# Where TensorE issues D·xs and the sums over states in a selective-scan kernel

## The chip, the cores and the metric

The kernel runs on one core of a Trainium2 chip. A core has five engines that run side by side[...]: TensorE (PE in the profile, its weight loads PEld), VectorE (DVE), ScalarE (ACT), GpSimd (POOL) and SyncE (SP), which here issues every DMA. The metric is the device time of one execution in microseconds, as a median of several executions.

## The reference, cut to what matters

Two layers are computed on x of shape (2, 256, 256, 128) in float32. The first is an attention along rows, which the change leaves alone. The second is a selective scan (Mamba-like) over the 256 × 256 tokens of each of the two images, with 256 inner channels and 16 states a channel:

```python
dA  = exp(delta[:, :, :, None] * A[None, :, None, :])
dBx = (delta * xs)[..., None] * Bs            # along the tokens
h   = dA_t * h + dBx_t                        # the recurrence, one token after another
y_t = sum_n h[:, :, n] * c_t[:, n]            # sum over the 16 states
y   = y + Ds * xs
out = (layernorm(y) * silu(z)) @ out_proj_w.T # plus the residual
```

xs, z, Bs, Cs and delta come from the normalised input by a projection with a 3 × 3 depthwise convolution (one set of nine matmuls here), a SiLU and small projections.

## The kernel before, in words

After the attention, which takes the first 2.67 ms, comes the scan stage. It works through 128 **steps** (two images, 64 steps each); a step is 4 rows of 256 tokens, T = 1024 tokens. A step is cut into NU = 32 **units**, one per **slot** of the schedule: two halves h of 128 channels, in each four groups m of four states, in each four groups q of 32 channels. A unit fills 128 partitions with 32 channels × 4 states. So a half is 16 units (NM), and four consecutive units (NQ) share m.

For a unit t the engines do this:

- `decay` (ACT, L956): da = exp(delta · A), written one slot ahead. Two buffers, da0 and da1.
- `drive` (POOL, L966): hb = (delta·xs)·B for two units at once, three buffers.
- `scan` (DVE, L978): the recurrence over 1024 tokens.
- `product` (DVE, L992): yc = h · C, except for the pairs that `POOLED` names (units 2, 3, 6, 7, 10, 11, 18, 19, 26, 27 of a step), whose product `products` (L1001) does on POOL two slots later. yc has four buffers of two units each.
- `add_up` (PE, L1023): for four units at once, 16 matmul records with the constant matrix `sel` add the four states of yc into y in PSUM. For the first group of a half (m = 0) the old `add_up` first loads xr (the half's xs, L1012) and puts D·xs into y with a diagonal matrix (L1016, 4 records).
- `y_out` (ACT, L1036): y goes to SBUF after a half's last group.
- `remember` (ACT, L983): keeps the last column of h for the next step.

A product of unit t writes into a yc buffer that the group of units around t − 8 used; it waits until that group's `add_up` has read it.

Beside the units, each slot carries **pieces** of other work, placed by `at(...)`: the projection of a later step (`project`: transposes t_ps L658, convolution taps u_ps L676, z_ps L702, xd_ps L726, dt_ps L744, each followed one or more slots later by the ACT instruction that empties its PSUM buffer: xn L663, xs L687, sz L713, xd L739, delta L755) and the end of an earlier step (`finish_row`, one row of 256 tokens every 8 slots: yt L828, ACT statistics and scaling L840 to L852, yd L863, gating on DVE L871, o_ps L875 and L879, and the ACT copy ob L889). All the projection's PE pieces share one PSUM buffer (pool `ps_p`, bufs = 1), so each waits until ACT has emptied the one before. The finish pieces share another (`ps_f`).

The order on PE, ACT, DVE and POOL is written out by hand: inside `tc.manual_schedule` the loop over t issues, for each slot, what the body names, top to bottom, and each engine runs its own part in that order. Only SP, the queue of the DMAs, is ordered by the framework's scheduler. `slots` holds for each slot a pair of lists: pieces of other engines, and pieces of PE. In the old loop a slot's PE work was all pieces of PE first, then the sums. The sums of a group of units u to u+3 come in slot u+5, or u+6 if the last pair's product is POOL's. Counted within a step, the groups 0, 4, 8, 16 and 24 are summed in slots 6, 10, 14, 22 and 30; groups 12, 20 and 28 have no POOL product in their last pair and are summed in slots 17, 25 and 1 (of the next step). Slot 17 also holds a z_ps piece, slot 25 four transposes, slot 1 the second xd_ps piece. Groups 0 and 16 open a half, so D·xs stood in slots 6 and 22, directly ahead of the sums and behind the ninth convolution tap.

The PE pieces of slots 0 to 3, which the prediction follows, are: slot 0 yt and the first xd_ps; slot 1 the second xd_ps; slot 2 dt_ps; slot 3 the first three taps of a convolution. ACT empties the first xd_ps in slot 1, the second in slot 2, dt_ps in slot 3, in each case behind that slot's `decay` and the finish pieces, and ahead of `remember`:

```python
        for t, i in ((40, 0), (41, 1)):
            at(base + t, states, i, pe=True)
            at(base + t + 1, states_out, i)
```

Of the kernel before, what the change touches and what calls it, by code (L numbers as in the profile page):

```python
# [8 lines left out]
F32 = mybir.dt.float32  # L9
# [6 lines left out]
P = 128  # L16
# [5 lines left out]
def attn_then_ssm_kernel(  # L22
# [26 lines left out]
    nc = tc.nc  # L49
# [8 lines left out]
    TB = 512  # L58
# [63 lines left out]
    d_diag = const.tile([P, NH, P], F32, name="d_diag")  # L122
# [3 lines left out]
    NQ = P // CQ  # L126
# [7 lines left out]
    with tc.tile_pool(name="prep", bufs=1) as prep, tc.tile_pool(  # L134
        name="prep2", bufs=3
# [14 lines left out]
        for g in range(NCG):  # L150
            for m in range(NSG):
                nc.sync.dma_start(
                    out=alog_d[:, :, g, m],
                    in_=A_logs[g * CQ : (g + 1) * CQ, m * SR : (m + 1) * SR],
# [101 lines left out]
    with tc.tile_pool(name="st", bufs=1) as stp, tc.tile_pool(  # L256
        name="st_x", bufs=6
# [20 lines left out]
    with ExitStack() as actx:  # L278
# [242 lines left out]
        end = B * NA  # L521
# [59 lines left out]
    T = R * W  # L581
    NSTEP = H // R
    NB = T // TB
# [4 lines left out]
    NM = NQ * NSG  # L588

    POOLED = (2, 6, 10, 18, 26)  # L590
    s1 = ctx.enter_context(tc.tile_pool(name="s1", bufs=1))
# [5 lines left out]
    ps_y = ctx.enter_context(tc.tile_pool(name="ps_y", bufs=1, space=PSUM))  # L597
# [7 lines left out]
    slots = {}  # L605
# [9 lines left out]
    given = {}  # L615
# [296 lines left out]
    def unit(t):  # L912

        k, i = divmod(t, NU)
        h, i = divmod(i, NM)
        m, q = divmod(i, NQ)
        return k, h, m, q
# [3 lines left out]
    def fetch(t):  # L921
        k, h, m, q = unit(t)
        v = given[k]
        if q == 0:

            for name, row in (("bb", m * SR), ("cc", NS + m * SR)):
                tl = repeats[name, k, h, m] = s2.tile([P, T], F32, name=name)
                nc.sync.dma_start(
                    out=tl, in_=v["bc"][row : row + SR, :].partition_broadcast(CQ)
                )  # L930
        if m == 0:

            for name in ("delta", "du"):
                if name == "delta":
                    tl = s5.tile([P, T], F32, name="delta_r")
                elif q % 2 == 0:
                    pair = spreads["pair", k, h, q] = s3.tile([P, 2, T], F32, name="du_r")
                    tl = pair[:, 0, :]
                else:
                    tl = spreads["pair", k, h, q - 1][:, 1, :]  # L940
                spreads[name, k, h, q] = tl
                nc.sync.dma_start(
                    out=tl,
                    in_=v[name][h, q * CQ : (q + 1) * CQ, :]
                    .unsqueeze(1)
                    .to_broadcast([CQ, SR, T]),
                )

    def pooled(t):
        return t % NU - t % 2 in POOLED  # L950

    def decay(t):
        k, h, m, q = unit(t)
        da = units[t]["da"] = ps_d.tile([P, T], F32, name=f"da{t % 2}")
        g = h * NQ + q
        nc.scalar.activation(  # L956
            da, spreads["delta", k, h, q], AF.Exp, scale=a_neg[:, g, m : m + 1]
        )

    def drive(t):  # L960

        k, h, m, q = unit(t)
        hb = s3.tile([P, 2, T], F32, name="hb")
        units[t] = {"pair": hb, "hb": hb[:, 0, :]}
        units[t + 1] = {"hb": hb[:, 1, :]}
        nc.gpsimd.tensor_tensor(  # L966
            hb,
            spreads["pair", k, h, q],
            repeats["bb", k, h, m].unsqueeze(1).to_broadcast([P, 2, T]),
            ALU.mult,  # L970
        )

    def scan(t):
        k, h, m, q = unit(t)
        u = units[t]
        st = states_of[steps[k][0]][:, h * NQ + q, m : m + 1]
        u["h"] = u["hb"] if pooled(t) else u["da"]
        nc.vector.tensor_tensor_scan(u["h"], u["da"], u["hb"], st, ALU.mult, ALU.add)  # L978

    def remember(t):  # L980
        k, h, m, q = unit(t)
        st = states_of[steps[k][0]][:, h * NQ + q, m : m + 1]
        nc.scalar.copy(st, units[t]["h"][:, T - 1 : T])  # L983

    def product(t):
        k, h, m, q = unit(t)
        u = units[t]
        if t % 2 == 0:
            yc = s4.tile([P, 2, T], F32, name="yc")
            for i in range(2):  # L990
                units[t + i]["yc"] = yc[:, i, :]
        nc.vector.tensor_tensor(u["yc"], u["h"], repeats["cc", k, h, m], ALU.mult)  # L992

    def products(t):

        k, h, m, q = unit(t)
        hb = units[t]["pair"]
        yc = s4.tile([P, 2, T], F32, name="yc")
        for i in range(2):
            units[t + i]["yc"] = yc[:, i, :]  # L1000
        nc.gpsimd.tensor_tensor(  # L1001
            yc, hb, repeats["cc", k, h, m].unsqueeze(1).to_broadcast([P, 2, T]), ALU.mult
        )

    outs = {}

    def add_up(t):

        k, h, m, _ = unit(t)
        if m == 0:  # L1010
            xr = s1.tile([P, T], F32, name="xr")
            nc.sync.dma_start(out=xr, in_=given[k]["xs"][h])  # L1012
            y = outs["y"] = ps_y.tile([P, T], F32, name="y")
            for i in range(NB):
                cols = slice(i * TB, (i + 1) * TB)
                nc.tensor.matmul(  # L1016
                    y[:, cols], d_diag[:, h, :], xr[:, cols], start=True, stop=False
                )
        y = outs["y"]
        for i in range(NB):  # L1020
            cols = slice(i * TB, (i + 1) * TB)
            for q in range(NQ):
                nc.tensor.matmul(  # L1023
                    y[q * CQ : (q + 1) * CQ, cols],
                    sel,
                    units[t + q]["yc"][:, cols],
                    start=False,
                    stop=(m == NSG - 1),
                )
        for q in range(NQ):  # L1030
            del units[t + q]

    def y_out(t):
        k, h, _, _ = unit(t)
        ys[k, h] = s2.tile([P, T], F32, name=f"ys{h}")
        nc.scalar.copy(ys[k, h], outs["y"])  # L1036
# [4 lines left out]
    end = len(steps) * NU  # L1041
# [7 lines left out]
    with tc.manual_schedule(engines=engines):  # L1049
        for t in range(min(slots), max(slots) + 1):  # L1050
            if 0 <= t + AHEAD < end:
                fetch(t + AHEAD)
            if 0 <= t < end and t % (NU * NSTEP) == 0:
                st = s1.tile([P, NCG, NSG], F32, name="state")
                nc.gpsimd.memset(st, 0.0)
                states_of[steps[t // NU][0]] = st
            if 0 <= t + 3 < end and t % 2:
                drive(t + 3)
            if 0 <= t - 2 < end and t % 2 == 0 and pooled(t - 2):
                products(t - 2)  # L1060
            if 0 <= t + 1 < end:
                decay(t + 1)
            if 0 <= t < end:
                scan(t)
                if not pooled(t):
                    product(t)
            if 0 <= t - 7 < end and unit(t - 7)[2:] == (NSG - 1, 0):
                y_out(t - 7)
            for pieces in slots.pop(t, ()):
                for piece, args in pieces:  # L1070
                    piece(*args)
            for u in (t - 6, t - 5):
                if 0 <= u < end and u % NQ == 0 and (u == t - 6) == pooled(u + NQ - 1):
                    add_up(u)
            if 0 <= t < end:
                remember(t)

# [36 lines left out]
```

## Time and profile before

| | us |
|---|---|
| median of 3 executions | 16321.47 (16320.95 to 16323.75) |
| the profiled execution | 16311.47 |
| its span | 16309.7 |
| scan stage, first scan to last scan | 2671.6 to 16251.3 |
| DVE busy in the span | 14627.3 (90%) |
| PE busy | 13759.1 (84%) |
| POOL busy | 13051.0 (80%) |
| ACT busy | 10765.8 (66%) |

Inside the scan stage the shares are higher than over the span: from 8000 to 9000 us DVE is busy for 957, POOL for 940, PE for 835 and ACT for 693 us of 1000. The profile's granted TensorE clock has two values in this kernel, 1.0 and 0.5; its mean over the span is 0.941. A row of the table of groups names line, engine, operation and tiles, then the count, the busy time in us and the mean of one in ns, then the engine's idle time just before such instructions and what ended most of it. In the timeline a row is start, duration, the instruction, and in brackets the idle time before it with its releaser.

### The profile page before, as it was taken

To read this page: it belongs to the slowest core of one execution; us is meant where nothing else is said; L and a number is where in the kernel's file an instruction comes from. 1 tells how busy PE (TensorE), PEld (TensorE's weight loads), DVE (VectorE), ACT (ScalarE), POOL (GpSimd) and SP (SyncE) were. 2 spreads that over 40 slices of the span, in tenths; PEclk is the share of its full clock that TensorE was granted. 3 is DMA by queue.
4 is the path that set the end of the run, shared out by engine and by line. 5 is a ranking of instruction groups with operands and counts; after the bars stand their busy time and mean duration, and the time that the engine had idled before them with its cause. 6 is when DMAs were issued, how large, how long until landed. Compare 5 with 4: busy or idle time off the path is not lost. (4 is left out here: it accounts for less than half of the span.)

```text
span 16309.7 us, 178677 instructions
## 1 busy us (share of the span) xinstructions
PE 13759.1 (84%) x59451; PEld 7060.9 (43%) x59451; DVE 14627.3 (90%) x12484; ACT 10765.8 (66%) x20003; POOL 13051.0 (80%) x3216
## 2 busy tenths in 40 slices
PE   6999997888888888888888888888888888888886
PEld 5877883333333333333333333333333333333333
DVE  7665555999999999999999999999999999999998
ACT  3555554666666666666666666666666666666665
POOL 0111114999999999999999999999999999999997
PEclk8999998999999999999999999999999999999998
DMA  4322223666666666666666666666666666666665
GB/s 184 133 90 79 92 78 142 239 233 233 240 235 230 236 233 233 236 239 231 230 236 234 230 234 231 235 232 234 238 238 231 231 234 234 235 240 233 228 237 179
DMA packets 1428912, 3452.16 MB, mean 212 GB/s; under 512 B 119784, under 2 KB 711184, under 8 KB 1407504
## 3 DMA queue, kind: packets, MB, share of 16 engines
q1 hardware_dynamic: 1427984, 3440.73, 60.6%
q8 instruction: 467, 7.65, 0.2%
q14 instruction: 461, 3.78, 0.1%
HBM read 2752.41 MB, written 687.88 MB: 211 GB/s over the span
## 5 line engine op out<-in xcount | busy, mean ns | idle before, releaser
L966 POOL TENSOR_TENSOR hb<-du_r,bb 128x2048 f32<-128x2048 f32 x2048 | 9259.2, 4545 | 521.8 <-DVE da L978 456.4
L978 DVE TENSOR_TENSOR_SCAN da<-da,state,hb 128x1024 f32<-128x1024 f32 x2816 | 6606.2, 2346 | 137.4 <-ACT da L956 134.5
L676 PE MATMUL u_ps<-xn,w_tap 128*128 128x512 f32 x9216 | 4537.7, 641 | 657.4 <-ACT sz L713 433.7
L956 ACT ACTIVATE da<-delta_r,a_neg 128x1024 f32<-128x1024 f32 x4096 | 4588.3, 1120 | 93.0 <-ACT state L983 1.5
L992 DVE TENSOR_TENSOR yc<-da,cc 128x1024 f32<-128x1024 f32 x2816 | 3449.1, 1225 | 439.3 <-PE y L1023 277.0
L1001 POOL TENSOR_TENSOR yc<-hb,cc 128x2048 f32<-128x2048 f32 x640 | 2902.2, 4535 | 346.0 <-DVE hb L978 176.7
L676 PEld LDWEIGHTS u_ps<-xn,w_tap 128*128 128x128 f32 x9216 | 1792.6, 204 | 3099.4 <-issue 2065.9
L978 DVE TENSOR_TENSOR_SCAN hb<-da,state,hb 128x1024 f32<-128x1024 f32 x1280 | 2959.8, 2338 | 113.0 <-ACT da L956 113.0
L983 ACT COPY state<-da 128x1 f32<-128x1 f32 x2816 | 447.5, 159 | 3103.2 <-DVE yc L992 3094.6
L1023 PE MATMUL y<-yc,sel 128*32 128x512 f32 x16384 | 2192.7, 654 | 18.1 <-POOL yc L1001 18.1
L435 POOL TENSOR_TENSOR x1g<-xc,bo_all 128x512 f32<-128x512 f32 x256 | 315.7, 1274 | 1839.8 <-DVE stats L484 1838.9
L828 PE MATMUL yt<-centre,ys 128*128 128x256 f32 x4096 | 1067.1, 405 | 610.1 <-ACT ob L889 610.1
L385 ACT ACTIVATE e<-s_ps,nmx 128x256 f32<-128x256 f32 x1024 | 477.0, 475 | 968.6 <-DVE nmx L376 952.4
L828 PEld LDWEIGHTS yt<-centre,ys 128*128 128x128 f32 x4096 | 762.0, 196 | 797.7 <-ACT ob L889 707.5
L1023 PEld LDWEIGHTS y<-yc,sel 128*32 128x32 f32 x16384 | 452.6, 115 | 1499.1 <-issue 1318.1
L744 PE MATMUL dt_ps<-xd,w_dt 8*128 8x512 f32 x1024 | 685.4, 754 | 227.6 <-ACT delta L755 128.9
L702 PE MATMUL z_ps<-xn,w_z 128*128 128x512 f32 x1024 | 568.2, 636 | 332.3 <-ACT sz L713 241.2
L879 PE MATMUL o_ps<-w_out,szr 128*128 128x128 f32 x4096 | 798.0, 277 | 0.0
L879 PE MATMUL o_ps<-w_out,yg 128*128 128x128 f32 x4096 | 797.4, 277 | 0.0
L352 DVE TENSOR_TENSOR v<-v_ps,bv_all 128x512 f32<-128x512 f32 x256 | 177.0, 692 | 590.8 <-PE v_ps L345 590.8
L879 PEld LDWEIGHTS o_ps<-w_out,yg 128*128 128x128 f32 x4096 | 668.7, 194 | 27.6
L773 POOL TENSOR_TENSOR xs<-delta,xs 128x1024 f32<-128x1024 f32 x256 | 598.8, 2364 | 97.3 <-ACT delta L763 97.3
(133 smaller groups left out, 16531.0 us busy)
## 6 DMA issues: line engine op xcount, KB each, us to landing
bb<-bc_d SPq DMA_DIRECT2D x1024, 512.0 KB, 4.6
cc<-bc_d SPq DMA_DIRECT2D x1024, 512.0 KB, 4.1
delta_r<-delta_d SPq DMA_DIRECT2D x1024, 512.0 KB, 6.0
du_r<-du_d SPq DMA_DIRECT2D x1024, 512.0 KB, 5.5
sz_d<-sz SPq DMA_DIRECT2D x128, 1024.0 KB, 6.8
szr<-sz_d SPq DMA_DIRECT2D x512, 256.0 KB, 5.4
xs_d<-xs SPq DMA_DIRECT2D x128, 1024.0 KB, 8.7
xr<-xs_d SPq DMA_DIRECT2D x256, 512.0 KB, 5.4
```

Source lines behind the costliest of these rows:

```text
L676: nc.tensor.matmul(o["u"], w_tap[:, h, tap, :], xn[:, i * RB + dy : i * RB + dy + RB, dx : dx + W], start=(tap == 0), stop=(tap == 8),)
L702: nc.tensor.matmul(o["z"], w_z[:, h, :], xn[:, 1 + i * RB : 1 + (i + 1) * RB, 1 : W + 1], start=True, stop=True,)
L744: nc.tensor.matmul(o["dt"], w_dt[:, h, :], o["xd"][0:DR, i * TB : (i + 1) * TB], start=True, stop=True,)
L773: nc.gpsimd.tensor_tensor(du, o["delta"][:, h, :], du, ALU.mult)
L828: nc.tensor.matmul(o["yt"][:, j, :], ys[k, h][:, t0 + j * P : t0 + (j + 1) * P], centre[:, (1 - h) * P : (1 - h) * P + DI], start=(h == 0) ...
L879: nc.tensor.matmul(o["o"][:, j, :], o[by][:, h, j * P : (j + 1) * P], w_out[:, i, h, :], start=False, stop=(j == WT - 1 and h == NH - 1 an ...
L956: nc.scalar.activation(da, spreads["delta", k, h, q], AF.Exp, scale=a_neg[:, g, m : m + 1])
L966: nc.gpsimd.tensor_tensor(hb, spreads["pair", k, h, q], repeats["bb", k, h, m].unsqueeze(1).to_broadcast([P, 2, T]), ALU.mult,)
L978: nc.vector.tensor_tensor_scan(u["h"], u["da"], u["hb"], st, ALU.mult, ALU.add)
L992: nc.vector.tensor_tensor(u["yc"], u["h"], repeats["cc", k, h, m], ALU.mult)
L1001: nc.gpsimd.tensor_tensor(yc, hb, repeats["cc", k, h, m].unsqueeze(1).to_broadcast([P, 2, T]), ALU.mult)
L1023: nc.tensor.matmul(y[q * CQ : (q + 1) * CQ, cols], sel, units[t + q]["yc"][:, cols], start=False, stop=(m == NSG - 1),)
```

## The change

Two things move on PE; nothing is added to the computation and nothing is left out.

- D·xs and its load leave `add_up` for a new `start_up`, which is issued in slot 5 (and 21) behind that slot's PE pieces, one slot earlier than before. That puts it ahead of the ninth tap of the convolution, which is in slot 6 (and 22).
- Sums of a group whose last pair has no POOL product (slots 17, 25, 1) are issued ahead of the slot's PE pieces instead of behind them. Sums with a POOL product stay behind the pieces.

```diff
+    def start_up(t):
+
+        k, h, _, _ = unit(t)
+        xr = s1.tile([P, T], F32, name="xr")
+        nc.sync.dma_start(out=xr, in_=given[k]["xs"][h])
+        y = outs["y"] = ps_y.tile([P, T], F32, name="y")
+        for i in range(NB):
+            cols = slice(i * TB, (i + 1) * TB)
+            nc.tensor.matmul(y[:, cols], d_diag[:, h, :], xr[:, cols], start=True, stop=False)
+
     def add_up(t):
 
-        k, h, m, _ = unit(t)
-        if m == 0:
-            xr = s1.tile([P, T], F32, name="xr")
...
+        _, _, m, _ = unit(t)
         y = outs["y"]
...
-            for pieces in slots.pop(t, ()):
-                for piece, args in pieces:
-                    piece(*args)
-            for u in (t - 6, t - 5):
-                if 0 <= u < end and u % NQ == 0 and (u == t - 6) == pooled(u + NQ - 1):
-                    add_up(u)
+            others, on_pe = slots.pop(t, ((), ()))
+            for piece, args in others:
+                piece(*args)
+            if 0 <= t - 5 < end and (t - 5) % NQ == 0 and not pooled(t - 2):
+                add_up(t - 5)
+            for piece, args in on_pe:
+                piece(*args)
+            if 0 <= t - 5 < end and (t - 5) % NM == 0:
+                start_up(t - 5)
+            if 0 <= t - 6 < end and (t - 6) % NQ == 0 and pooled(t - 3):
+                add_up(t - 6)
```

The order on ACT, DVE and POOL is the same in both kernels. On SP some DMAs change places once a step: the store of xs (xs_d, L698), which stood ahead of a load of bb (L928), is issued behind it; a load of delta_r moves ahead of a load of cc, and the store of the output row ahead of the load of xres.

More of the change, by code (lines that the diff above doesn't have):

```diff
@@ L1005, in attn_then_ssm_kernel @@
     outs = {}
-    def add_up(t):
-        k, h, m, _ = unit(t)
-        if m == 0:
-            xr = s1.tile([P, T], F32, name="xr")
[L1012 to L1018, printed above, removed]
+    def start_up(t):
[6 more added lines that the diff above has]
+            nc.tensor.matmul(y[:, cols], d_diag[:, h, :], xr[:, cols], start=True, stop=False)
+    def add_up(t):
+        _, _, m, _ = unit(t)
         y = outs["y"]
```

## The prediction

> **What bounds the kernel now.** I read the table of groups first. In the scan stage DVE has the most work, and its rows name its waits:
>
> ```profile
> L978 DVE TENSOR_TENSOR_SCAN da<-da,state,hb 128x1024 f32<-128x1024 f32 x2816 | 6606.2, 2346 | 137.4 <-ACT da L956 134.5
> L992 DVE TENSOR_TENSOR yc<-da,cc 128x1024 f32<-128x1024 f32 x2816 | 3449.1, 1225 | 439.3 <-PE y L1023 277.0
> L978 DVE TENSOR_TENSOR_SCAN hb<-da,state,hb 128x1024 f32<-128x1024 f32 x1280 | 2959.8, 2338 | 113.0 <-ACT da L956 113.0
> ```
>
> So 277 us of waiting for sums on PE and some 115 us (in the scan stage) for da are all that an order on PE can win. The timeline says where: in nearly every step three waits stand, before the products of units 8 and 12 (for y) and the scan of unit 11 (for da). One step, which begins (first scan) at 8394.15 and whose successor begins at 8499.48:
>
> ```profile
> 8420.88 1.22 DVE L992 TENSOR_TENSOR yc<-da,cc 128x1024 f32<-128x1024 f32 x1 [0.61 <-PE y L1023]
> 8428.72 2.35 DVE L978 TENSOR_TENSOR_SCAN hb<-da,state,hb 128x1024 f32<-128x1024 f32 x1 [0.82 <-ACT da L956]
> 8434.28 1.23 DVE L992 TENSOR_TENSOR yc<-da,cc 128x1024 f32<-128x1024 f32 x1 [0.95 <-PE y L1023]
> ```
>
> The sums waited for are those of slots 6 and 10. What makes them late starts in slot 0. PE, then ACT, in that step:
>
> ```profile
> 8397.86 1.93 PE L726 MATMUL xd_ps<-xs,w_xp 128*64 128x512 f32 x4
> 8400.46 1.93 PE L726 MATMUL xd_ps<-xs,w_xp 128*64 128x512 f32 x4 [0.67 <-ACT xd L739]
> 8402.32 1.92 PE L1023 MATMUL y<-yc,sel 128*32 128x512 f32 x16
> 8404.17 1.12 PE L744 MATMUL dt_ps<-xd,w_dt 8*128 8x512 f32 x2
> 8407.15 4.54 PE L676 MATMUL u_ps<-xn,w_tap 128*128 128x512 f32 x6 [1.86 <-ACT delta L755]
> ```
>
> ```profile
> 8402.93 0.20 ACT L848 ACTIVATE rstd<-lve 128x2 f32<-128x2 f32 x1
> 8403.04 0.56 ACT L739 COPY xd<-xd_ps 64x512 f32<-64x512 f32 x1
> 8403.63 0.19 ACT L983 COPY state<-hb 128x1 f32<-128x1 f32 x1
> 8403.73 1.11 ACT L956 ACTIVATE da<-delta_r,a_neg 128x1024 f32<-128x1024 f32 x1
> 8404.78 1.00 ACT L1036 COPY ys<-y 128x1024 f32<-128x1024 f32 x1
> 8405.68 0.83 ACT L852 ACTIVATE yn<-yt,rstd 128x256 f32<-128x256 f32 x2
> 8406.40 0.69 ACT L755 ACTIVATE delta<-dt_ps,dtb_c 128x512 f32<-128x512 f32 x1
> ```
>
> The convolution of slot 3 starts 13.00 us into the step, when ACT has emptied dt_ps; ACT had no idle time on the way. From there PE works without a gap through yd, nine more taps, D·xs and the sums of slot 6 (end 8420.84), so that the product of unit 8 is late; and o_ps, ob, yt, dt and delta follow from it, PE and ACT in turn, until the sums of slot 10 end. That chain doesn't ask DVE for anything. Behind the product of unit 12 only DVE's own work is left: from its start to the next step's first scan I find 65.20 us in all but a few steps.
>
> The windows view shows the second ingredient (us, busy times, then the granted clock in the eighth column):
>
> ```profile
> 8403.70:8407.20 3.50, 1.64 (x11) 0.35 (x3) 3.50 (x2) 3.50 (x8) 2.20 (x2) 1.00 0.32 64
> 8407.20:8410.60 3.40, 3.40 (x4) 1.45 (x5) 3.31 (x3) 2.13 (x3) 3.39 (x1) 0.50 0.28 110
> 8431.10:8434.50 3.40, 3.40 (x17) 0.74 (x10) 2.45 (x2) 2.15 (x5) 3.40 (x2) 0.50 0.94 287
> ```
>
> After a stretch in which PE had little to do its clock is halved, and six taps take 4.54 us instead of 2.84.
>
> [...] half-clock stretches are 3.41, 6.8 or 10.24 us long, on one grid through the kernel. [...] leaving the 8-row dt matmuls out: a full-clock window with under 0.4 of PE time was followed by a half one in all 220 cases, one with over 0.6 in none; out of the half state only windows of about 0.77 and more led. [...]
>
> **Why the windows matter.** 31 windows are 31 × 3.413 = 105.81 us. From the first scans of steps 4 to 126 I get 43 steps of 105.3 (to 105.7), 58 of 106.4, 10 of 107.7, 7 of 105.9; mean 106.20, and 106.08 without two disturbed ones (119.0, where the image changes, and 106.9). The short ones have a window edge 2.6 to 2.9 us after their start, the long ones 3.05 to 3.5: there a second half-clock window falls on the dt pieces of slots 8 to 10, and the product of unit 12 comes 28.19 instead of 27.14 us after the convolution's start. 13.00 + 27.14 + 65.20 = 105.34; 13.00 + 28.19 + 65.20 = 106.39. A short step moves the edge 0.47 us later, a long one 0.58 earlier; they alternate, and the pair loses 0.1 us on the grid until the edge comes under 2.59, where yt and the first xd_ps run at half clock and two or three steps (105.9, 106.4, 107.7) slip a whole window.
>
> **The change, part by part.**
>
> *Sums ahead of the second xd_ps (slot 1).* The sums follow the first xd_ps at once (8399.72) and take 1.85 us until the next can start; their yc is ready, unit 31's product having ended before the step began. So the second xd_ps starts at 8401.57 (now 8400.46) and ends at 8403.50. ACT, which now takes it at 8403.04 without waiting, takes it 0.04 us after its end (as it does for the first): 8403.54, so 0.50 later. dt_ps starts 0.05 after ACT's copy: 8404.15, as now (8404.17); before, the sums covered that wait. But ACT's queue behind the copy is full: da, ys, yn and delta each shift by 0.50, and the convolution starts at 13.50. Unit 4's da ends 11.2 us into the step, its scan begins at 11.64: nobody else is hit. In the steps with a half clock in slot 0 (29 of 123) the same sum gives 1.13: first xd_ps to 7.28, second to 11.00, ACT at 11.04 instead of 9.91.
>
> *D·xs a slot earlier.* 4 records, 1.88 us, twice a step, change places with a tap of 0.45 us. PE is busy without a gap from the fourth tap to the end of the sums, so the sums end when they did: 0. The cover is the tap itself; y was emptied 10 us before, and xr lands 5.4 us after its issue, half a step ahead. SP: xr's load keeps its neighbours. xs_d (1 MB, 8.7 us to land) now waits behind a bb load that waits for POOL; its reader xr comes some 80 us later. The cc load behind it starts at most 8.7 us later, but its first reader is the product of unit 4, 14.06 us into the step: 0.
>
> *Sums ahead of z_ps (slot 17) and of the transposes (slot 25).* Each fills a wait of PE for ACT (1.66 and 2.27 us) and no product waited for these sums: no gain. z_ps starts about 0.2 us later, its reader ACT two microseconds after it. But the idle time is gathered: the window at 60.9 to 64.3 us holds 1.13 us of work (0.33), so the taps of slot 19 start at half clock, that window holds 0.53, and the next stays half. They lose (71.12 − 65.89)/2 = 2.6 us; the sums of slot 22 end at 80.5, and the product of unit 24, their waiter, starts at 81.85. Hidden by 1.3 us. ACT's slots 24 to 26 follow 2.2 us later, and the da of units 26, 27 and 28 then come 0.8, 0.25 and 0.28 us before their scans: 0, with little cover.
>
> **The sum.** Cheapest step: 13.50 + 27.14 + 65.20 = 105.84. With the edge 2.6 to 2.9 us after the start, hence 2.75 to 3.05 after the convolution's, fewer taps run at half clock: a step whose convolution began at 13.37 shows 27.04, so 105.74. Between lies 105.81, 31 windows. A step that is shorter moves the edge later and makes the next longer, and the other way round: the steps should lock to 105.81 and never slip. 123 × (106.20 − 105.81) = 48 us, less 14 for the two disturbed steps, which stay: 34 us. The profiled execution would give 16277; the median stands 10 us above it, so 16321.5 − 34 = 16287.
>
> **Rivals.** *No lock, the delay paid in full*: 94 × 0.50 + 29 × 1.13 = 80 us, or 16401. It decides once the cheapest step exceeds 105.81, which needs only 0.15 us more in ACT's queue (convolution at 13.65 instead of 13.50), for example from the thin cover in slots 26 to 28. For it: every number in the queue is tight. *The slip goes on, cheaper or dearer by little*: one window lost in 10 to 12 steps gives 105.81 + 3.41/11 = 106.12, 16311 to 16340. It comes if the convolution starts before 13.47, so that the edge creeps later until it meets the long steps. *The change removes the waits for y*: 2.2 us a step, 270 us, 16050. Against it: the sums of slots 6 and 10 stand behind the same work as before.
>
> **How the numbers follow.** Lock 0.38, paid in full 0.30, slip goes on 0.25, waits removed 0.02, worse than any of these 0.05. A measurement here tells 0.2% (33 us) from nothing. The lock lies at that bound, so a good two thirds of it count as faster; the slip is mostly the same; the second rival is slower. Faster 0.28, same 0.34, slower 0.38. The range, 16265 to 16410, holds the lock with some luck and the second rival; the likeliest case alone is 16265 to 16305.
>
> **What would show it.** Right: the second xd_ps behind the sums, ACT's xd L739 waiting for PE xd_ps L726 in most steps (now 49 us in all), convolutions 13.5 us into the step, and nearly all steps 105.8 long, half-clock stretches at fixed places in the step. Wrong: a convolution start off 13.50, new DVE waits in slots 4 or 26 to 28, or step lengths still alternating.

## The result and the profile after

| | median, us | ratio to the kernel before (95%) |
|---|---|---|
| before | 16321.97 (16320.95 to 16323.75) | |
| changed | 16346.40 (16333.21 to 16366.62) | 1.0016 (0.9999 to 1.0033) |

So the median rose by 0.16%, and the interval of the ratio still holds 1: a loss of this size is just not told from nothing. The time lies inside the range that was forecast (16265 to 16410), but not where the likeliest case put it (16287). The profiled execution of the changed kernel took 16366.62 us with a span of 16364.8, the dearest of the four; its steps average 106.62 us (steps 4 to 126) against 106.20 before.

The DVE rows of the table of groups after (columns as before; `add_up`'s sums are L1024 now):

```profile
L978 DVE TENSOR_TENSOR_SCAN da<-da,state,hb 128x1024 f32<-128x1024 f32 x2816 | 6606.1, 2346 | 141.9 <-ACT da L956 139.7
L992 DVE TENSOR_TENSOR yc<-da,cc 128x1024 f32<-128x1024 f32 x2816 | 3449.1, 1225 | 487.1 <-PE y L1024 326.8
L978 DVE TENSOR_TENSOR_SCAN hb<-da,state,hb 128x1024 f32<-128x1024 f32 x1280 | 2960.0, 2338 | 114.2 <-ACT da L956 114.2
```

The waits of DVE for y did not shrink, they grew from 277 to 327 us, which is 50 of the 55 us by which the spans differ. They still stand before the products of units 8 and 12, but not as before: the wait before unit 8 grew from 73 to 144 us, and the one before unit 12 fell from 205 to 183. A common step of the changed kernel begins at 7032.62 and lasts 105.74 us. Its PE timeline, then ACT's:

```profile
7036.33 1.93 PE L726 MATMUL xd_ps<-xs,w_xp 128*64 128x512 f32 x4
7038.19 1.92 PE L1024 MATMUL y<-yc,sel 128*32 128x512 f32 x16
7040.05 1.93 PE L726 MATMUL xd_ps<-xs,w_xp 128*64 128x512 f32 x4
7042.65 1.12 PE L744 MATMUL dt_ps<-xd,w_dt 8*128 8x512 f32 x2 [0.67 <-ACT xd L739]
7046.00 4.42 PE L676 MATMUL u_ps<-xn,w_tap 128*128 128x512 f32 x6 [2.23 <-ACT delta L755]
```

```profile
7041.41 0.20 ACT L848 ACTIVATE rstd<-lve 128x2 f32<-128x2 f32 x1
7042.02 0.58 ACT L739 COPY xd<-xd_ps 64x512 f32<-64x512 f32 x1 [0.40 <-PE xd_ps L726]
7042.50 0.19 ACT L983 COPY state<-hb 128x1 f32<-128x1 f32 x1
7042.59 1.12 ACT L956 ACTIVATE da<-delta_r,a_neg 128x1024 f32<-128x1024 f32 x1
7043.64 1.00 ACT L1037 COPY ys<-y 128x1024 f32<-128x1024 f32 x1
7044.55 0.83 ACT L852 ACTIVATE yn<-yt,rstd 128x256 f32<-128x256 f32 x2
7045.27 0.68 ACT L755 ACTIVATE delta<-dt_ps,dtb_c 128x512 f32<-128x512 f32 x1
```

The second xd_ps starts 7.43 us into the step, ACT takes it at 9.40, and has waited 0.40 us for it. The convolution starts at 13.38, not at 13.50. And the steps are not all alike: 66 of 123 last 105.6 or 105.7 us, 15 last 106.8 or 106.9, 11 last 107.2 to 107.3, 25 last 108.0 to 108.8. Three first scans in a row of the DVE timeline, with steps of 107.23 and 107.99 us between them:

```profile
7561.24 2.35 DVE L978 TENSOR_TENSOR_SCAN da<-da,state,hb 128x1024 f32<-128x1024 f32 x1
...
7668.47 2.35 DVE L978 TENSOR_TENSOR_SCAN da<-da,state,hb 128x1024 f32<-128x1024 f32 x1
...
7776.46 2.35 DVE L978 TENSOR_TENSOR_SCAN da<-da,state,hb 128x1024 f32<-128x1024 f32 x1
```

So the change paid 0.38 us on the critical queue of ACT in an ordinary step, and the lock of the steps at 31 windows (105.81 us), which should have paid that back, did not come. A window is one cell of the grid of 3.4133 us on which the half-clock stretches of these profiles begin: none of the 390 stretches of the kernel before and the 535 of the changed one starts more than 0.001 us off it. Averaged over steps 4 to 124 of the two profiles the convolution starts only 0.16 us later (13.46 in place of 13.30), since yt and the first xd_ps run at half clock in 6 steps in place of 29; another 0.25 us is lost behind it, from its start to the product of unit 12 (27.83 in place of 27.58).

### The profile page after: what moved, and what is told of

Read it like the earlier page. It is cut to its first block, busy times and chain, and to the rows that moved or that the text cites. A ratio compares the mean times of both kernels' runs of the same rounds, so it can differ in the third digit from the quotient of the medians.

```text
span 16364.8 us, 178796 instructions
## 1 busy us (share of the span) xinstructions
PE 14102.2 (86%) x59451; PEld 7209.7 (44%) x59451; DVE 14625.1 (89%) x12484; ACT 10765.1 (66%) x20003; POOL 13046.0 (80%) x3216
## 5 line engine op out<-in xcount | busy, mean ns | idle before, releaser
L676 PE MATMUL u_ps<-xn,w_tap 128*128 128x512 f32 x9216 | 5005.0, 691 | 718.1 <-ACT sz L713 433.9
L676 PEld LDWEIGHTS u_ps<-xn,w_tap 128*128 128x128 f32 x9216 | 1941.9, 221 | 3379.7 <-issue 2273.1
L1024 PE MATMUL y<-yc,sel 128*32 128x512 f32 x16384 | 2191.9, 654 | 18.0 <-POOL yc L1001 18.0
L1024 PEld LDWEIGHTS y<-yc,sel 128*32 128x32 f32 x16384 | 451.9, 114 | 1475.6 <-issue 1221.9
L744 PE MATMUL dt_ps<-xd,w_dt 8*128 8x512 f32 x1024 | 646.8, 715 | 322.8 <-ACT delta L755 139.7
L889 ACT COPY ob<-o_ps 128x256 f32<-128x256 f32 x512 | 189.3, 370 | 860.8 <-PE o_ps L879 827.7
```

The lines of the kernel that those rows point to most:

```text
L676: nc.tensor.matmul(o["u"], w_tap[:, h, tap, :], xn[:, i * RB + dy : i * RB + dy + RB, dx : dx + W], start=(tap == 0), stop=(tap == 8),)
L744: nc.tensor.matmul(o["dt"], w_dt[:, h, :], o["xd"][0:DR, i * TB : (i + 1) * TB], start=True, stop=True,)
L1024: nc.tensor.matmul(y[q * CQ : (q + 1) * CQ, cols], sel, units[t + q]["yc"][:, cols], start=False, stop=(m == NSG - 1),)
```

## The experiments

The theory: the copy of the second xd_ps on ACT sets the start of slot 3's convolution, that start sets the product of unit 12, and the mean step is then decided by how step lengths stand to 31 windows. The rivals are named in each expectation.

### Which part of the change costs

*D·xs alone.* From the changed kernel, the sums of slots 17, 25 and 1 go back behind the pieces:

```diff
-            if 0 <= t - 5 < end and (t - 5) % NQ == 0 and not pooled(t - 2):
-                add_up(t - 5)
             for piece, args in on_pe:
                 piece(*args)
+            if 0 <= t - 5 < end and (t - 5) % NQ == 0 and not pooled(t - 2):
+                add_up(t - 5)
```

> D xs one slot earlier alone, all sums behind the slot's pieces. Theory (the copy of the second xd_ps on ACT sets the start of slot 3's convolution, D xs costs nothing): convolution 13.00 us into an ordinary step, steps of 105.3 and 106.4 us in turn, as before: 16310 to 16335 us. Rival (D xs between two taps breaks PE's run or the DMA order costs): sums of slot 6 later than 13.73 us after the convolution's start, or steps longer; 16345 us and more.

Measured: 16319.62 us, ratio 1.0002 (0.9993 to 1.0010). Convolution at 13.00, steps of 105.3 and 106.4, unit 8's product 13.73 us after the convolution in 96 of 121 steps, all as before. D·xs a slot earlier costs nothing and wins nothing.

*Slot 1 alone, and slots 17 and 25 alone.* In the kernel before, the sums go first only in the slots named, here slot 1; the other kernel has `(17, 25)`:

```diff
+            early = t % NU in (1,) and 0 <= t - 5 < end
+            others, on_pe = slots.pop(t, ((), ()))
+            for piece, args in others:
+                piece(*args)
+            if early:
+                add_up(t - 5)
+            for piece, args in on_pe:
+                piece(*args)
...
+                if early and u == t - 5:
+                    continue
```

> Only the sums of slot 1 go ahead of the second xd_ps; D xs and the sums of slots 17 and 25 stay as before. Theory: convolution at 13.38 us, cheap steps of 105.73 us that let the window edge creep later until the steps of 106.8 to 108.3 us come; as long as the whole change, 16330 to 16375 us. Rival (the sums of slots 17 and 25, with the half clock in slot 19, make the loss): 16320 us as before.

> Only the sums of slots 17 and 25 go ahead of the pieces; slot 1 and D xs stay as before. Theory: convolution at 13.00 us; half clock from 64 to 71 us of the step, hidden (no wait of DVE before the product of unit 24); cheap steps 105.34 us, 16290 to 16330 us, below before if the later o_ps of slot 31 spares yt its half clock. Rival (that half clock reaches DVE): waits for da before the scans of units 26 to 28, steps longer by 0.3 us or more, 16360 us.

Measured: slot 1 alone 16369.75 us, ratio 1.0034 (1.0021 to 1.0047); slots 17 and 25 alone 16298.15 us, ratio 0.9990 (0.9983 to 0.9996). The two rivals fall: all the loss is slot 1's, and the other two slots win 20 us. Against the kernel before of the same session the parts make +51 and -20 us, together +31; the whole change made +24, and its four executions lie 33 us apart. The DVE rows of the table of groups tell the same, slot 1 alone first:

```profile
L978 DVE TENSOR_TENSOR_SCAN da<-da,state,hb 128x1024 f32<-128x1024 f32 x2816 | 6604.8, 2345 | 172.9 <-ACT da L956 170.1
L992 DVE TENSOR_TENSOR yc<-da,cc 128x1024 f32<-128x1024 f32 x2816 | 3448.0, 1224 | 477.8 <-PE y L1023 317.4
```

```profile
L978 DVE TENSOR_TENSOR_SCAN da<-da,state,hb 128x1024 f32<-128x1024 f32 x2816 | 6604.7, 2345 | 137.8 <-ACT da L956 135.4
L992 DVE TENSOR_TENSOR yc<-da,cc 128x1024 f32<-128x1024 f32 x2816 | 3448.1, 1224 | 429.7 <-PE y L1023 267.7
```

With slot 1 alone the convolution starts at 13.4 in 89 of 121 steps and at 15.0 in 30, those with a half clock in slot 0; in these the scan of unit 4 waits for da (36 us in all). With slots 17 and 25 alone it stays at 13.00, the clock is half 67.5 us into the step in 120 of 121 steps (16 of 121 with D·xs alone), and DVE's waits don't grow by it (267.7 us for y and 135.4 for da, before 277.0 and 134.5). What they win: yt and xd_ps of slot 0 meet the half clock in 9 steps of 121 instead of 29. In the changed kernel o_ps of slot 31 ends later, 0.3 us after the step's start in the step above (7032.94), so that the window ahead of yt holds more work; that this is the reason is argued, not tried by itself. The size fits: the mean start of the convolution falls from 13.30 to 13.10 us, the mean from there to the product of unit 12 stays (27.58 and 27.59), and 0.20 us × 123 steps is 25 us.

### Does the lock exist?

The cheapest step of the changed kernel is 0.07 us short of 31 windows. So adding work to the critical queue should make it faster. The same edit with 1, 2 and 4 copies on the changed kernel and 3 and 5 on the kernel before; `pad` and `ln_eps` are 128x1:

```diff
+    pad = s1.tile([P, 1], F32, name="pad")
...
         def size_out(h, i):
...
+            if (h, i) == (0, 0):
+                for _ in range(1):
+                    nc.scalar.copy(pad, ln_eps)
```

> The changed kernel with one copy of 128x1 more on ACT in slot 3, ahead of the copy that empties dt_ps: the convolution of slot 3 starts 0.1 to 0.19 us later. Theory of the lock: 13.48 to 13.57 us is inside the range in which the steps hold at 105.81 us: 16280 to 16305 us, against 16346 us without the copy. Rival (paid step by step): 16358 to 16370 us.

> The changed kernel with two copies of 128x1 more on ACT in slot 3, ahead of the copy that empties dt_ps. They do nothing but delay the convolution of slot 3 by 0.2 to 0.35 us. Theory of the lock: with a delay of 0.08 to 0.22 us the cheap step is over 105.81 us, the steps stay at 105.81 us, and the kernel gets faster by work added: 16280 to 16300 us; with 0.25 us or more it slips again, 16340 to 16390 us. Rival (no lock; the delay is paid step by step): 16346 + 123 x 0.2 to 0.35 = 16370 to 16390 us.

> The changed kernel with four such copies: the convolution 0.4 to 0.75 us later, beyond the range of the lock. Theory: every step is longer than 105.81 us, the window edge runs earlier all the time and the dear steps come often: 16370 to 16430 us. Rival (the delay is hidden): 16346 us.

> The kernel before with three copies of 128x1 more on ACT in slot 3: the convolution at 13.5 to 13.6 us (five copies: 13.98). Theory of the lock: inside 13.46 to 13.64 us the kernel before holds at 105.81 us a step as the changed kernel did with one copy: 16280 to 16305 us, faster than without the copies. Rival (the lock needs the changed order too, or the delay is paid): 16322 + 123 x 0.55 = 16390 us.

> The kernel before with five such copies in slot 3: the convolution 0.45 to 0.95 us later than 13.00. Theory of the lock: at 13.47 to 13.64 us the kernel before locks as well, 16275 to 16300 us, faster than 16322 by five instructions added to its critical queue; beyond 13.64 it slips, 16340 to 16400 us. Rival (paid step by step): 16377 to 16440 us.

| kernel | convolution at, us | commonest steps, us | median, us | ratio to before (95%) |
|---|---|---|---|---|
| changed | 13.38 | 105.7 (56 of 123) | 16346.40 | 1.0016 (0.9999 to 1.0033) |
| changed, 1 copy | 13.46 | 105.8 (110) | 16290.91 | 0.9982 (0.9975 to 0.9990) |
| changed, 2 copies | 13.69 | 105.9, 106.0 (91), 108.5, 108.6 (22) | 16373.65 | 1.0035 (1.0022 to 1.0048) |
| changed, 4 copies | 14.13 | 108.8, 109.0 (69), 106.5 (28) | 16568.85 | 1.0150 (1.0133 to 1.0167) |
| before, 3 copies | 13.5 | 105.8 (93) | 16332.22 | 1.0006 (0.9998 to 1.0015) |
| before, 5 copies | 13.98 | 106.3 (54), 108.7 (48) | 16500.09 | 1.0109 (1.0094 to 1.0124) |

One copy more, and the kernel is 55 us faster than without it: its slowest execution took 16304.39 us, the fastest without the copy 16333.21. The tile `pad` isn't the cause, for the kernels with two and four copies have it too. The first scans, from the DVE timeline, stand 105.81 us apart, step after step:

```profile
7018.23 2.35 DVE L982 TENSOR_TENSOR_SCAN da<-da,state,hb 128x1024 f32<-128x1024 f32 x1
...
7124.04 2.35 DVE L982 TENSOR_TENSOR_SCAN da<-da,state,hb 128x1024 f32<-128x1024 f32 x1
...
7229.85 2.35 DVE L982 TENSOR_TENSOR_SCAN da<-da,state,hb 128x1024 f32<-128x1024 f32 x1
```

Its ACT timeline shows how little was added, 0.08 us between the start of the copy and that of delta:

```profile
7030.87 0.19 ACT L758 COPY pad<-ln_eps 128x1 f32<-128x1 f32 x1
7030.95 0.69 ACT L759 ACTIVATE delta<-dt_ps,dtb_c 128x512 f32<-128x512 f32 x1
```

Each copy after the first costs 0.22 us, and beyond the lock the time rises faster than the delay: two more copies after the second add 195 us for 0.44 us × 123 = 54. The profiles show where that comes from: in the changed kernel a half-clock stretch of two windows lies across the convolution (it begins 12 to 14 us into the step) in 19 of 121 steps; with one copy in 2, with two in 24, with four in 80, and in 63 with five copies on the kernel before.

The expectations fared unevenly. One copy came where the lock was expected. For two copies both ranges hold 16373.65, so that it decides nothing: the common steps are longer by the delay (106.0 us), and steps over 106.6 are fewer than without copies (27 of 123 in place of 52). Four copies and five took 16569 and 16500 us, dearer than the lock's slip (at most 16430 and 16400) and dearer than the delay paid step by step or hidden: how much the slip costs there was not foreseen. Three copies on the kernel before came between the two ranges.

The kernel before with three copies is half a miss. It locks too, with 93 steps of 105.8 us in the profiled execution, so the lock doesn't need the changed order. It is also where the steps are seen to be pulled back. Where the second image begins, four first scans in a row (DVE timeline, the lines between left out) are 105.90, 105.87 and 105.84 us apart, and steps of 105.82 and 105.81 follow. Meanwhile the first window edge behind the start of a step comes at 3.03, 2.95, 2.89 and 2.87 us, and then stays at 2.86:

```profile
9477.36 2.36 DVE L982 TENSOR_TENSOR_SCAN da<-da,state,hb 128x1024 f32<-128x1024 f32 x1 [0.41 <-POOL state L1059]
9583.26 2.35 DVE L982 TENSOR_TENSOR_SCAN da<-da,state,hb 128x1024 f32<-128x1024 f32 x1
9689.13 2.35 DVE L982 TENSOR_TENSOR_SCAN da<-da,state,hb 128x1024 f32<-128x1024 f32 x1
9794.97 2.35 DVE L982 TENSOR_TENSOR_SCAN da<-da,state,hb 128x1024 f32<-128x1024 f32 x1
```

The changed kernel with one copy shows no such pull: its steps last 105.80 to 105.81 us wherever the window edge stands between 2.87 and 3.15 us, and the edge creeps later by 0.005 us a step in place of 0.07. It gains because its step all but equals 31 windows, not because anything holds it there.

The kernel before with three copies isn't faster than without them: steps of 107.4 to 108.7 us, by which it is thrown out of the lock, take back what the lock gives. Most of what throws it out is on record. Between steps 4 and 124 DVE stalls five times for 0.44 to 0.46 us before a product, with nothing in the profile that ended the wait: in steps 6, 24, 71, 88 and 106, in this kernel, in the changed one with one copy, and in the two without copies alike. Here, with the edge held at 2.86 us, each of the five begins a fall (a sixth, in step 82, has no such stall). In the changed kernel with one copy the edge stood at 2.96 to 3.17 us in these steps, and only the stall of step 71 ended in a slip. What the stalls are stays open.

### What the chain to unit 12 is worth

*y_out one slot later.* In slots 4 and 20 ACT waits for DVE anyway:

```diff
-            if 0 <= t - 7 < end and unit(t - 7)[2:] == (NSG - 1, 0):
-                y_out(t - 7)
+            if 0 <= t - 8 < end and unit(t - 8)[2:] == (NSG - 1, 0):
+                y_out(t - 8)
```

> The kernel before with y_out one slot later (slots 4 and 20 in place of 3 and 19), where ACT waits for DVE anyway. Theory (ACT's queue from slot 2 to the copy of dt_ps sets the chain to the product of unit 12): convolution at about 12.1 us in place of 13.00, steps of 104.4 to 105.5 us, waits of DVE before units 8, 11 and 12 smaller by 0.9 us a step: 16180 to 16230 us. Rival (the chain is set elsewhere): 16322 us.

> The changed kernel with y_out one slot later. Theory: its convolution starts 0.9 us earlier too, at 12.5 us, so 16346 - 123 x 0.9 = 16235 us, give or take 40 us for where the steps fall on the clock's windows; dearer than the kernel before with the same edit (16176 us) by the 0.38 us of slot 1. Rival (the order of slot 1 costs nothing once y_out is out of the way): 16176 us.

Measured: 16176.11 us on the kernel before, ratio 0.9909 (0.9895 to 0.9924); 16276.73 us on the changed kernel, ratio to before 0.9972 (0.9961 to 0.9983). On the kernel before the convolution starts at 12.1, the wait before unit 8 is gone and that before unit 11 falls from 100 to 25 us: that ACT's queue sets the chain is shown. The time is just below what was expected. The wait before unit 12 did not get smaller (213 us, before 205): a half-clock stretch of 6.8 us or more now begins 33 to 34 us into 99 of 121 steps, in place of 66, and the product of unit 12 comes up to 28.3 us after the convolution. On the changed kernel the gain is 70 us instead of 111, just outside what was expected (16195 to 16275): 98 of its 123 steps last 105.8 us. It is held at 31 windows, from the other side: in steps 30 to 59 those of 105.79 us, with yt and the first xd_ps at half clock, change about with those of 105.84 or 105.85, without, and the window edge stays between 2.57 and 2.62 us. And it now waits for da before unit 4 (68 us). The whole change costs 100 us there; that all of it is slot 1's was not tried.

*Sums of slot 10 first.* If the sums for unit 12 are late because of what stands ahead of them, these are the sums to move. The edit is that of slot 1, for slot 10:

```diff
...
+            if t % NU in (10,):
+                for u in sums:
+                    add_up(u)
+                sums = []
             for piece, args in on_pe:
                 piece(*args)
...
```

> The kernel before with the sums of slot 10 ahead of that slot's dt piece; all else as before. Their products are ready by 30.1 us of the step, and PE waits 0.8 to 1.1 us before each dt piece. Theory (the product of unit 12 waits for these sums only because they stand behind the dt piece that waits for ACT): the wait before unit 12 (199 us in all) nearly gone, those before units 8 and 11 stay, steps of 104.5 to 104.9 us: 16110 to 16170 us. Rival (dt, pushed back by the sums, delays ACT and with it the da of units 11 to 14): no gain, 16300 us and more.

> Both that helped together, on the kernel before: the sums of slots 10, 17 and 25 ahead of the pieces, and y_out one slot later. Theory: the waits before units 8, 11 and 12 (368 us in all) nearly gone, steps of 103.2 to 103.8 us: 15990 to 16060 us. Rival (another engine becomes the bound, POOL with 100.1 us of work a step first): waits for POOL before scans, 16100 us and more.

Measured: 16148.59 us, ratio 0.9894 (0.9879 to 0.9908), and together with y_out later and slots 17 and 25 16019.27 us, ratio 0.9816 (0.9802 to 0.9831). That is faster than both kernels, by 300 us than the one before in the same session. The DVE rows of the table of groups of the two kernels, slot 10 first alone and then both together:

```profile
L978 DVE TENSOR_TENSOR_SCAN da<-da,state,hb 128x1024 f32<-128x1024 f32 x2816 | 6606.9, 2346 | 181.7 <-ACT da L956 174.2
L992 DVE TENSOR_TENSOR yc<-da,cc 128x1024 f32<-128x1024 f32 x2816 | 3449.1, 1225 | 230.2 <-PE y L1023 50.6
```

```profile
L992 DVE TENSOR_TENSOR yc<-da,cc 128x1024 f32<-128x1024 f32 x2816 | 3449.1, 1225 | 188.8 <-DMA cc<-bc_d 6.3
L978 DVE TENSOR_TENSOR_SCAN hb<-da,state,hb 128x1024 f32<-128x1024 f32 x1280 | 2949.9, 2335 | 26.1 <-ACT da L956 23.6
```

The wait for y falls from 277 to 51 us, and in the last kernel it is no longer among the releasers that the row names. A part comes back, as the rival of the first had it: dt now follows the sums, and the scan of unit 13 waits 38 us in all for its da, the scan of unit 3 another 21. 49 of the 123 steps of the last kernel take 103.2 us, where DVE's own work is 101.7; POOL did not become the bound, for DVE's scans wait some 2 us in all for it.

## Why the prediction was right, and where it was not

*The range*: right, with some luck. It spans from the lock to the delay paid in full, so it left room for almost any case; the case held likeliest (0.38) did not come, and the one that came, the slip goes on (0.25), was sized 16311 to 16340, below the measured 16346. Of its own signs the second xd_ps behind the sums came, and ACT's wait for it (135 times in place of 65); convolutions at 13.50 and steps all of 105.8 us did not, and of its signs of being wrong a start off 13.50 and unequal step lengths did.

*The bound and the chain*: right. In every profile but those that move the sums of slot 10 the product of unit 12 stood 65.2 us before the next step, in 113 or more of 121 steps. That the sums of slots 6 and 10 would go on making DVE wait was right too. That sums behind a piece which waits for ACT wait with it, on which the argument rests, is shown for slot 10: issued ahead of that slot's dt piece they left 50.6 us of waiting for y in place of 277.0.

*D·xs a slot earlier, 0*: right, 1.0002 measured alone. Its working took one record for a tap, which is two: the ninth takes 0.95 us (7056.71 to 7057.66 in the changed kernel), not 0.45, the "six taps" at half clock are three, and behind yd six more follow, not nine. The sum doesn't hang on it.

*Slots 17 and 25, 0*: the half clock came where it was put (64.4 to 71.2 us) and was hidden. What the step missed is the small gain in slot 0, 20 us.

*Slot 1, 0.50 us*: this is the term that was mis-sized. Second xd_ps at 7.42 and ACT at 9.39 were worked out; 7.43 and 9.40 came. But the queue behind it was not as full as the prediction said. Before, the xd copy ended at 8403.60 and the state copy behind it began at 8403.63; after, it ended at 7042.60 and the state copy began at 7042.50, 0.10 us ahead of that end. Before, the state copy had still to wait for the scan of unit 2, which ended at 8403.60; after, that scan had ended half a microsecond earlier. So the delay ate 0.12 us, and 0.38 was left. The convolution came at 13.38 and the cheapest step at 13.38 + 27.16 + 65.20 = 105.74, 0.07 us under 31 windows. The edge then crept later by 0.07 us a step until it met the long steps.

*The lock*: half right. Steps can be held at 31 windows, as the kernel before with three copies (93 of 123 steps of 105.8 us) and the changed kernel with y_out later (98 of 123) show, while the changed kernel missed it by those 0.07 us. With one copy more it came to 16291, where the prediction had put 16287; but there the steps were not pulled to 31 windows, they were 31 windows long by the size of the copy, so that this agreement is luck in part. The prediction named the way to miss the lock (a convolution before 13.47) as its third case. That case was priced too low because its dear steps were taken from the kernel before. In the changed kernel the half clock at the convolution spans two windows in 19 of 121 steps (in most of these 12.8 to 19.6 us into the step), and the dearest steps last 108.0 to 108.8 us instead of 107.7. That the longer wait of PE ahead of the convolution (2.23 us in place of 1.86) brings this about is argued, not tried.

*The delay paid in full, 16401*: the whole change did not show it. Slot 1 alone came near it once the sizes are put right: its convolution starts 0.38 us later in ordinary steps and 0.8 us (15.0 in place of 14.2) in the 30 that still run slot 0 at half clock, 0.48 in the mean; that makes 59 us, and 51 were measured. So for that kernel the time doesn't tell the slip from the delay paid.

*The clock*: that PE's load in a window sets the clock of the next was the author's reading; the counts that it stands on were nearly right. Counted again over the scan stage of the kernel before, without the dt matmuls, 282 of 285 full-clock windows with under 0.4 of PE time were followed by a half one, and none of 2654 with over 0.6; with the dt matmuls counted, 141 windows with 0.5 to 0.77 were. Three half-clock stretches were longer than 10.24 us (13.7 to 23.9).

## What to carry to other kernels

A matmul group that stands behind a waiting piece is not always better off ahead of it: ask who reads the piece that is pushed back. Here the sums filled a wait of PE that was free (0.67 us) and took away the cover under which ACT emptied the next buffer (slot 1 alone lost 51 us); the sums that DVE did wait for, in slot 10, were the ones worth moving (171 us won). And in this kernel the half-clock stretches began on a grid of 3.4133 us, and steps near 31 of its cells stayed at 105.8 us or slipped, so that a tenth of a microsecond a step decided a third of a per cent (16346.40 or 16290.91 us): look for such a grid in the granted clock before a change of that size is explained by its own cost.

## What the runs showed of the hardware

- The half-clock stretches began on one grid of 3.4133 us through the whole of a profile: a straight line through their starts misses none by more than 0.001 us (390 stretches of the kernel before, 535 of the changed kernel).
- A copy of 128x1 added to ScalarE's critical queue, which started the convolution 0.08 us later, made the kernel 55 us faster (16346.40 to 16290.91): 110 of 123 steps then lasted 105.8 us, which is 31 such windows.
- Copies of 128x1 in a row, into one tile, ahead of an activation on ScalarE: the first put the convolution off by 0.08 us (13.38 to 13.46), two by 0.31 (13.69), four by 0.75 (14.13), so each after the first by 0.22. With four a step the middle one of the 512 records took 0.191 us.
- In the changed kernel the half clock that began 64.0 to 67.4 us into a step lasted through a second window in 121 of 121 steps. The first of the two held 0.34 to 0.72 of PE time (0.61 in the middle, without the dt matmuls). Of all half-clock windows of that scan stage after which the clock was full again, the emptiest held 0.78.
- Full-clock windows with 0.5 to 0.6 of PE time, counted the same way, were followed by a full-clock one in all 42 cases of the changed kernel and in 265 of 266 of the kernel before.
